# First layer's expert outputs stored by slot, and gathered per token in the second layer, in a two-layer graph network kernel

## The chip, the core and the metric

The kernel runs on one core of one Trainium2 chip. The core has a tensor engine for matrix products (PE), a vector engine (DVE), a scalar engine (ACT), a general engine (POOL), a sync engine that mostly starts transfers (SP), and 16 DMA engines that carry the transfers. The metric is the device time of one execution in microseconds (us); the median of several runs is compared. All data is float32 unless a line says otherwise.

## The reference, cut to what matters

625 nodes (called tokens here) with 768 features pass through two layers. Each layer adds a graph convolution and a linear-attention mix to x, and then a mixture-of-experts network in which each token goes to 2 of 8 experts:

```python
xn = _layernorm(x)
x = x + _L0_gnn_ref(xn, ...) + _L0_mix_ref(xn, ...)        # layer 0
x = x + _L0_ffn_ref(_layernorm(x), ...)                    # experts of layer 0
xn = _layernorm(x)
x = x + _L1_gnn_ref(xn, ...) + _L1_mix_ref(xn, ...)        # layer 1
x = x + _L1_ffn_ref(_layernorm(x), ...)
return x

def _L0_ffn_ref(x, Wg, bg, W1, b1, W2, b2, W3, b3):
    scores = x @ Wg + bg
    topk_vals, topk_idx = jax.lax.top_k(scores, 2)
    gates = softmax(topk_vals)
    comb = einsum('bnk,bnke->bne', gates, one_hot(topk_idx, 8))
    out = zeros_like(x)
    for e in range(8):
        h = gelu(x @ W1[e] + b1[e])          # 768 -> 192
        h = gelu(h @ W2[e] + b2[e])          # 192 -> 384
        y = h @ W3[e] + b3[e]                # 384 -> 768
        out = out + comb[..., e:e+1] * y
    return out
```

The change touches the last line of the expert network of layer 0, that is, how each token's two gated outputs y are added to x, and the first lines of layer 1, which take the layernorm of that sum.

## The kernel before

Tokens are kept as NB = 5 blocks of T = 125 rows. A list scheduler orders each engine's instructions; where the text of the program asks for it, the vector engine is kept in the written order (L1185 to `in_order.close` at L1211, ahead of the expert blocks). Every engine works through its own instructions strictly in that order.

The experts of layer 0 work on slots. The router chooses two experts per token, and `Dispatch` gives each of the 1250 token-expert pairs a slot: `two_i` holds, for each token, its two slot numbers. The slots form 21 blocks, each for one expert: 13 blocks of 128 rows (NPB = 13) and 8 half blocks of 64. The list `RUN` has the 13 blocks that always run (0 to 9 among the whole ones, and the half blocks 13, 14 and 15, with 9 the last); the list `MORE` has the other eight, which run only if the routing fills them (`tc.If`, L1339). With these inputs it does not.

A block (`block0`, or `block0_half` for half blocks) loads the expert's weights on the sync queue, gathers its tokens' rows from the DRAM tensor `tokens` by an indirect transfer on POOL's queue (L532, tile `xg`), transposes them, makes three matrix products with two activations between, and multiplies the result by the gate (L1274, L1324, tile `y`, 128 x 768). Then y is added into the DRAM tensor `sums`, row by row at its tokens' places, by an indirect transfer on POOL's queue that reads, adds and writes (`scatter_add`, L536). `sums` holds x with the expert biases already, stored at L1213. As every scatter reads and writes the same tensor, each waits for the one before it. Half blocks put their two column halves on partitions 0 to 63 and 64 to 127, so their y has 128 x 384 elements. Two blocks are in work at a time (`blocks0`), each doing a step in turn; tiles `y` are two.

Behind the blocks a few transposes of a matrix of edge counts run (L1347). Then layer 1 starts (L1360 to L1367). For each token block b, the sync queue loads its rows of `sums` into a tile `part` (`token_rows` L367, in two transfers of 112 and 13 rows; three such tiles take turns), a layernorm is done on DVE (L243 to L232), the tensor engine transposes the block (L187), ACT or DVE copies the columns out (L177, L175), a matrix product with the graph convolution's first weights follows (L201), and a second layernorm and its transposes feed the mix. Later in layer 1 the rows of `sums` are loaded once more (L1548), for the residual. The `tc.If` that stands between the two layers makes the first load of layer 1 wait for all that was begun before it, on every queue.

The second graph convolution of layer 0 runs its eight relations in a loop and calls `vectors_of_features(r)` at each; this loads small parameter rows at r = 0, and transposes them at r = 1.

Of the kernel before, what the change touches and what calls it, by code (L numbers as in the profile page):

```python
# [7 lines left out]
F32 = mybir.dt.float32  # L8
BF16 = mybir.dt.bfloat16
I32 = mybir.dt.int32  # L10
# [7 lines left out]
T = 125  # L18
NB = 5
NH = 313  # L20
NP = 2 * NH
HC = 314
D = 768
# [9 lines left out]
NPB = 13  # L33
NHB = 8
NS = NPB + NHB
RUN = (0, 1, 2, 13, 3, 4, 5, 14, 6, 7, 8, 15, 9)
MORE = (10, 11, 12, 16, 17, 18, 19, 20)
# [6 lines left out]
def kernel(ctx: ExitStack, tc: tile.TileContext, a: dict, out: bass.AP):  # L44
    nc = tc.nc

    const = ctx.enter_context(tc.tile_pool(name="const", bufs=1))
    wpool = ctx.enter_context(tc.tile_pool(name="wpool", bufs=5))
    rowp = ctx.enter_context(tc.tile_pool(name="rowp", bufs=3))
    small = ctx.enter_context(tc.tile_pool(name="small", bufs=2))  # L50
    psum = ctx.enter_context(tc.tile_pool(name="psum", bufs=4, space=PSUM))
    dram = ctx.enter_context(tc.tile_pool(name="dram", bufs=1, space=DRAM))
# [174 lines left out]
    def layernorm(src, dst, width, blocks=range(NB), into=None):  # L227

        into = into or blocks
        mv, r = moments(src, width, blocks)  # L230
        for i, b in enumerate(blocks):
            nc.vector.tensor_scalar(dst[:, into[i], :], src[:, b, :], mv[:, i, 0:1], r[:, i : i + 1],  # L232
                                    op0=OP.subtract, op1=OP.mult)
# [53 lines left out]
    class Router:  # L287
# [52 lines left out]
        def add_biases(self, x, pool):  # L340
# [10 lines left out]
            for bs in ((0, 1, 2), (3, 4)):  # L351
# [6 lines left out]
                for b in bs:  # L358
                    nc.vector.tensor_add(halves(x[:, b, :]), pss[b][:T, :, :384], halves(x[:, b, :]))

    def token_rows(dram_ap, tile_ap, store):

        for p in (slice(0, 112), slice(112, T)):
            if store:
                nc.sync.dma_start(dram_ap[p], tile_ap[p])
            else:
                nc.sync.dma_start(tile_ap[p], dram_ap[p])  # L367

    def by_token(d):
        return d[0 : N, :].rearrange("(b p) d -> p b d", p=T)  # L370

    class Dispatch:
# [7 lines left out]
        def __init__(self, pool, keep, router):  # L380
# [5 lines left out]
            for b in range(NB):  # L386
                n = NB - b
# [30 lines left out]
            nc.vector.tensor_reduce(two[:, 1, :], pos, AX.X, OP.max)  # L418
            nc.vector.tensor_reduce(two[:, 0, :], pos, AX.X, OP.add)
            nc.vector.tensor_sub(two[:, 0, :], two[:, 0, :], two[:, 1, :])  # L420
            two_i = pool.tile([T, 2 * NB], I32, name="d_twoi", bufs=1)
            nc.vector.tensor_copy(two_i, two.rearrange("p c b -> p (c b)"))
            part_i = pool.tile([T, 2, 2 * NB], I32, name="d_parti", bufs=1)
            nc.vector.tensor_single_scalar(part_i[:, 0, :], two_i, 127, op=OP.bitwise_and)
# [28 lines left out]
            for k, of in enumerate((slice(0, NPB), slice(NPB, NS))):  # L453
                n = of.stop - of.start
# [76 lines left out]
    def gather(dst, table_d, rows):  # L531
        nc.gpsimd.indirect_dma_start(out=dst, out_offset=None, in_=table_d,  # L532
                                     in_offset=bass.IndirectOffsetOnAxis(ap=rows, axis=0))

    def scatter_add(table_d, src, rows):
        nc.gpsimd.indirect_dma_start(out=table_d, out_offset=bass.IndirectOffsetOnAxis(ap=rows, axis=0),  # L536
                                     in_=src, in_offset=None, compute_op=OP.add)
# [10 lines left out]
    def half_rows(table_d):  # L548
        return table_d.rearrange("r (h d) -> (r h) d", h=2)


    sides = [slice(0, 64), slice(64, 128)]
# [38 lines left out]


    tokens_d = [dram.tile([SPARE + 128, D], F32, name=f"tokens{i}") for i in range(2)]
    sums_d = [dram.tile([SPARE + 128, D], F32, name=f"sums{i}") for i in range(2)]

    def over_degrees(r):
# [92 lines left out]
    with tc.tile_pool(name="big0", bufs=1) as big, ExitStack() as stack:  # L689
# [20 lines left out]
        with ExitStack() as phase:  # L710
# [85 lines left out]
            for hp in range(KC):  # L796
# [3 lines left out]
                for b0 in range(0, NB, 2):  # L800
                    n = min(2, NB - b0)
# [334 lines left out]
        with tc.tile_pool(name="rel2", bufs=1) as rel:  # L1136

            places = {}
            columns_of = {}

            def vectors_of_features(r):
                if r == 0:
                    many = places["all"] = rowp.tile([128, 1024], F32, name="row")
                    for c, (name, n, width) in enumerate((("L0_ffn_b1", 16, 96), ("L0_ffn_b2", 24, 128), ("L1_ffn_b1", 72, 128))):
                        nc.scalar.dma_start(many[:n, c * 128 : c * 128 + width], vector_rows(name, width))
                    at = 0
                    for name, n in (("L1_gnn_g1", 8), ("L1_gnn_be1", 8), ("L1_gnn_br1", 8), ("L1_mix_ln_in_g", KC),
                                    ("L1_mix_ln_in_b", KC), ("L1_mix_ln_out_g", KC), ("L1_mix_ln_out_b", KC)):
                        nc.scalar.dma_start(many[at : at + n, 384:512], vector_rows(name, 128))
                        places[name] = at  # L1150
                        at += n
                    places["n"] = at
                if r != 1:
                    return
                many, at = places.pop("all"), places.pop("n")
                ps = ps_tile()
                for c, (name, n, width) in enumerate((("fb1", 16, 96), ("fb2", 24, 128), ("gb1", 72, 128))):
                    nc.tensor.transpose(ps[:width, 0, c * 128 : c * 128 + n], many[:n, c * 128 : c * 128 + width], ident[:n, :n])
                    columns_of[name] = const.tile([width, n], F32, name=f"cols_{name}")
                    nc.vector.tensor_copy(columns_of[name], ps[:width, 0, c * 128 : c * 128 + n])  # L1160
                nc.tensor.transpose(ps[:, 0, 384 : 384 + at], many[:at, 384:512], ident[:at, :at])
                nc.vector.tensor_copy(vectors, ps[:, 0, 384 : 384 + at])

                for b in range(NB):
                    nc.gpsimd.dma_start(edges_d[b, :T, blk(b)], ident[:T, :T], accum_op=OP.add)

                far = rel.tile([T, NB], I32, name="far_i", bufs=1)
                nc.vector.tensor_scalar(far, token[:T], -1.0, None, op0=OP.mult)
                near = rel.tile([T, NB], I32, name="near_i", bufs=1)
                nc.vector.tensor_single_scalar(near, far, 127, op=OP.bitwise_and)  # L1170
                nf = rel.tile([T, NB], F32, name="near_f", bufs=1)
                nc.vector.tensor_copy(nf, near)
                nc.vector.tensor_scalar(token_parts[:, 1, :], nf, -1.0, None, op0=OP.mult)
                nc.vector.tensor_add(token_parts[:, 0, :], token[:T], nf)

            router = Router(0, "L0_ffn_Wg", "L0_ffn_bg", "L0_ffn_b3", None, None)

            def rows_done(x):
                t = token_place(work_place())
                router.rows_of = lambda b: (t, b)  # L1180
                router.tT = rel.tile([128, 18 * HC], F32, name="pair", bufs=1)[:, : KC * NP].rearrange("p (k n) -> p k n", k=KC)

                def one(b):
                    if b == NB - 1:
                        in_order.enter_context(tc.manual_schedule(engines={mybir.EngineType.DVE}))  # L1185
                    router.rows(x, b)
                    if b:
                        router.score(b - 1)

                return one  # L1190

            slabs_ = slab_tiles(a["L0_gnn_W2"][0], D, 3)
            nc.scalar.dma_start(by_token(aside_d[2]), x)
            x = rgcn(rel, parts, "L0_gnn_W2", False, {"cnt": cnt, "over": over, "w": slabs_}, lambda i: (work_place, features_place, x_place)[i](),
                     lambda: recall(2, x_place), vectors_of_features, rows_done)
            router.choose(0, NB - 1)
            router.score(NB - 1)
            router.choose(NB - 1, NB)
# [6 lines left out]
    with tc.tile_pool(name="msums", bufs=1) as msums:  # L1205
        msum = msums.tile([128, NB, DQ * 128], F32, name="msum")
        with tc.tile_pool(name="work0", bufs=2) as moe:
            places_of = Dispatch(moe, moe, router)
            idx, es_i, used = places_of.idx, places_of.es_i, places_of.used
# [20 lines left out]
            def block0(b, spare_pool=None):  # L1230
# [35 lines left out]
                y = moe.tile([128, D], F32, name="y")  # L1266
# [5 lines left out]
                if not gates:  # L1272
                    gates.extend(gate())
                nc.vector.tensor_scalar(halves(y), ps[:, :, :384], gates[0][:, b : b + 1], None, op0=OP.mult)  # L1274
                scatter_add(sums_d[0], y, idx[:, b : b + 1])

            def block0_half(b, w1, w2, w3):

                i = b - NPB
# [42 lines left out]
                if not gates:  # L1322
                    gates.extend(gate())
                nc.vector.tensor_scalar(y, ps[:, 0, :384], gates[1][:, i : i + 1], None, op0=OP.mult)  # L1324
                scatter_add(half_rows(sums_d[0]), y, places_of.idx2[:, i : i + 1])

            def blocks0(bs, spare_pool=None):

# [21 lines left out]
    with ExitStack() as phase:  # L1350
# [6 lines left out]
        nc.vector.memset(xnT[:, :, N:NP], 0.0)  # L1357
        xl = lay.tile([T, NB, 1024], F32, name="xl")

        for b in range(NB):  # L1360
            xb = part.tile([T, 1, D], F32, name="part", bufs=3)
            token_rows(by_token(sums_d[0])[:, b, :], xb[:, 0, :], False)
            layernorm(xb, xb, D, [0])
            block_to_columns(xb, xnT, KC, b, 0)
            evac(halves(xl[:, b, :]), token_matmul(xnT, w1_of, KC, b, 512), b)
            layernorm(xb, xb, D, [0])
            block_to_columns(xb, hT, KC, b, 0, (AF.Identity, places["L1_mix_ln_in_g"], places["L1_mix_ln_in_b"]))  # L1367
# [95 lines left out]
        nc.scalar.copy(halves(kvb), pkv[:, :, :384])  # L1463


        gT = lay.tile([128, 8, NP], F32, name="gT")
        arow = source_rows(al, 4)
        brow = row("L1_gnn_b1", 1024)
        wq = slabs(wqkv[:, 0:D], D, 3)
# [286 lines left out]
```

## Time and profile before

| | |
|---|---|
| runs | 2396.97, 2398.72, 2400.65 us; median 2398.72 |
| profiled execution | 2397.42 us; its span 2395.7 us; tensor engine clock granted 0.971 |
| PE busy | 2220.3 us, 93% of the span |
| DVE busy | 929.5 us, 39% |
| ACT busy | 277.8 us, 12% |
| POOL busy | 466.2 us, 19% |
| DMA | 311.21 MB in 152851 packets, 130 GB/s over the span |

The expert blocks of layer 0 take about 1360 to 1490 us of the span, the start of layer 1 about 1490 to 1580. In the rows of the profile, L532 is the line of the helper that issues the gathers, L536 that of the scatters, L367 that of the loads of token rows. "x26" is a number of instructions, and "idle before" the time that an engine waited just ahead of them, with what ended most of the wait. "SPq", "ACTq" and "POOLq" are the transfers that an engine issues, and "issue to landing" is the time from the issue until the data has arrived.

### The profile page before, as it was taken

To read this page: it belongs to the slowest core of one execution; us is meant where nothing else is said; L and a number is where in the kernel's file an instruction comes from. 1 tells how busy PE (TensorE), PEld (TensorE's weight loads), DVE (VectorE), ACT (ScalarE), POOL (GpSimd) and SP (SyncE) were. 2 spreads that over 40 slices of the span, in tenths; PEclk is the share of its full clock that TensorE was granted. 3 is DMA by queue.
4 is the path that set the end of the run, shared out by engine and by line. 5 is a ranking of instruction groups with operands and counts; after the bars stand their busy time and mean duration, and the time that the engine had idled before them with its cause. 6 is when DMAs were issued, how large, how long until landed. Compare 5 with 4: busy or idle time off the path is not lost. (4 is left out here: it accounts for less than half of the span.)

```text
span 2395.7 us, 25088 instructions
## 1 busy us (share of the span) xinstructions
PE 2220.3 (93%) x10262; PEld 1470.3 (61%) x10262; DVE 929.5 (39%) x1930; ACT 277.8 (12%) x579; POOL 466.2 (19%) x262
## 2 busy tenths in 40 slices
PE   7999989999999999999999687699999998699997
PEld 4666556777776567777776454355666555455554
DVE  7554133444343333443452521522765533511111
ACT  2111000000001100000000122211643200111110
POOL 1676533232220022222210021000000200011100
PEclk9999999999999999999999799899999999699999
DMA  9435395444422051111101699121003200679795
GB/s 357 96 54 56 67 273 136 121 129 130 126 76 79 7 191 59 64 59 54 34 1 52 207 301 280 39 73 72 1 1 131 73 13 13 248 296 358 285 391 195
DMA packets 152851, 311.21 MB, mean 130 GB/s; under 512 B 49087, under 2 KB 70723, under 8 KB 152689
## 3 DMA queue, kind: packets, MB, share of 16 engines
q1 hardware_dynamic: 91154, 232.46, 27.7%
q0 software_dynamic: 52208, 49.67, 10.5%
q10 hardware_dynamic: 9358, 27.30, 3.4%
q8 instruction: 87, 1.43, 0.2%
q14 instruction: 44, 0.35, 0.0%
HBM read 249.49 MB, written 63.58 MB: 131 GB/s over the span
## 5 line engine op out<-in xcount | busy, mean ns | idle before, releaser
L921 PE MATMUL ps<-cnt,parts 125*128 125x314 bf16 x2880 | 389.5, 298 | 9.8 <-DVEq L1107 8.4
L921 PEld LDWEIGHTS <-parts 125*128 125x128 bf16 x2880 | 282.1, 98 | 116.8 <-issue 11.1
L677 POOL DMA_INDIRECT table<-val,idx x80 | 159.6, 1996 | 131.0 <-DMA table<-val,idx 69.3
L969 PE MATMUL ps<-pair,w 128*128 128x314 f32 x504 | 137.5, 431 | 7.6 <-ACT pair L177 7.6
L943 POOL TENSOR_TENSOR features<-w 128x1152 f32<-128x1152 f32 x14 | 37.3, 2668 | 522.0 <-issue 348.0
L1624 PE MATMUL ps<-w,xT 128*128 128x384 f32 x360 | 126.2, 502 | 11.3 <-DVE xT L175 6.7
L969 PEld LDWEIGHTS ps<-pair,w 128*128 128x128 f32 x504 | 96.3, 191 | 46.1 <-ACT pair L177 8.1
L532 POOL DMA_INDIRECT xg<-tokens,d_idx x26 | 27.2, 1045 | 482.9 <-DVE gates L338 151.2
L1640 PE MATMUL ps<-w,hT 128*128 128x384 f32 x360 | 119.2, 487 | 0.0
L201 PE MATMUL ps<-w,hT 128*125 128x384 f32 x360 | 117.8, 486 | 0.0
L1624 PEld LDWEIGHTS ps<-w,xT 128*128 128x128 f32 x360 | 67.8, 195 | 56.2 <-DVE xT L175 8.2
L177 ACT COPY features<-ps 128x628 f32<-128x628 f32 (+1 forms) x15 | 10.5, 703 | 766.8 <-PE ps L921 766.0
L201 PEld LDWEIGHTS ps<-w,hT 128*125 128x125 f32 x360 | 67.1, 188 | 47.0
L1640 PEld LDWEIGHTS ps<-w,hT 128*128 128x128 f32 x360 | 67.5, 190 | 45.0
L1434 PE MATMUL ps<-xl,pT 125*125 125x256 f32 (+1 forms) x300 | 81.1, 427 | 12.4 <-ACT pT L177 8.8
L890 PE MATMUL ps<-w,features 128*125 128x384 f32 x240 | 82.9, 504 | 0.0
L975 DVE TENSOR_TENSOR pair<-ps,pair 128x628 f32<-128x628 f32 (+1 forms) x60 | 44.8, 746 | 97.5 <-PE ps L969 97.5
L1546 POOL TENSOR_TENSOR row<-row 128x768 f32<-128x768 f32 x1 | 2.1, 2094 | 395.7 <-DVE off L1412 395.7
L536 POOL DMA_INDIRECT sums<-y,d_idx x25 | 39.5, 1578 | 202.8 <-DMA sums<-y,d_idx 81.0
L201 PE MATMUL ps<-w,features 128*125 128x384 f32 x240 | 78.5, 487 | 0.0
L210 PE MATMUL ps<-features,w 128*128 128x313 f32 x288 | 77.4, 427 | 0.0
L1434 PEld LDWEIGHTS ps<-xl,pT 125*125 125x125 f32 x300 | 56.2, 191 | 34.2 <-ACT pT L177 10.3
(426 smaller groups left out, 3349.9 us busy)
## 6 DMA issues: line engine op xcount, KB each, us to landing
w<-in_L_ffn_w_dram SPq DMA_DIRECT2D x78, 1152.0 KB
w<-in_L_gnn_W_dram SPq DMA_DIRECT2D x34, 1152.0 KB
w<-in_L_ffn_W_dram SPq DMA_DIRECT2D x13, 1152.0 KB
table<-zero SPq DMA_DIRECT2D x32, 400.0 KB
cnt<-table POOLq DMA_DIRECT2D x16, 800.0 KB, 8.1
edges<-cnt POOLq DMA_DIRECT2D x8, 1600.0 KB, 16.3
w<-in_L_ffn_W_dram SPq DMA_DIRECT2D x13, 576.0 KB
w<-in_L_mix_W_qkv_dram SPq DMA_DIRECT2D x6, 1152.0 KB
```

Of the source, the lines that this page charges most:

```text
L201: nc.tensor.matmul(ps[:T, h, :width], xT[:, k, blk(b)], w_of(k)[:, h * width : (h + 1) * width], start=(k == 0), stop=(k == nk - 1))
L210: nc.tensor.matmul(ps[:width, h, :NH], w_of(k)[:, c0 : c0 + width], xT[:, k, h * NH : (h + 1) * NH], start=(k == 0), stop=(k == nk - 1))
L536: nc.gpsimd.indirect_dma_start(out=table_d, out_offset=bass.IndirectOffsetOnAxis(ap=rows, axis=0), in_=src, in_offset=None, compute_op=OP.add)
L677: scatter = nc.gpsimd.indirect_dma_start(out=table_of(g, j), out_offset=bass.IndirectOffsetOnAxis(ap=idx[:, j : j + 1], axis=0), in_=val[: ...
L890: nc.tensor.matmul(ps[:T, h, :384], aggs[:, k, blk(b)], w_of(k)[:, h * 384 : (h + 1) * 384], start=(k == 0), stop=(k == KC - 1))
L921: nc.tensor.matmul(ps[:, h, :HC], parts[:, b, i, k * 128 : (k + 1) * 128], cnt[:T, b, h * HC : (h + 1) * HC], start=(b == 0 and i == 0), s ...
L943: nc.gpsimd.tensor_add(wmix[:, 1], b11, b12)
L969: nc.tensor.matmul(ps[:, j, :HC], right[:, k, c : c + 128], left(k), start=(k == 0), stop=(k == K2 - 1))
L975: nc.vector.tensor_add(total, ps[:, :n, :HC], total)
L1434: nc.tensor.matmul(o, pT[:, j, :], xl[:, j, cols], start=(j == 0), stop=(j == NB - 1))
L1624: nc.tensor.matmul(ps[:, 0, :384], xT[:, k, :], w1_of(k)[:, q * 384 : (q + 1) * 384], start=(k == 0), stop=(k == KC - 1))
L1640: nc.tensor.matmul(ps[:, h, :384], hT[:, k, :], w2_of(k)[:, h * 384 : (h + 1) * 384], start=(k == 0), stop=(k == 8))
```

## The change

In layer 0 each block's y is no longer added into `sums`. It is stored, by a plain transfer, to a new DRAM tensor `rows` with one row per slot (21 x 128 rows of 768). Whole blocks use one transfer of 128 rows, half blocks two of 64 rows and 384 columns, all on POOL's queue, but for the last block, which uses ACT's queue. As tokens' slots may lie anywhere, the rows of blocks and half blocks that are not written are filled with zeros before, at r = 2 of the second graph convolution of layer 0: one DVE instruction makes a tile of zeros, and eight transfers of 384 KB and three of 192 KB on ACT's queue store it. The tile of slot numbers is kept from the dispatch (`slots_of`).

At the beginning of layer 1, for each token block b, the row of x with biases is loaded from `sums`, two indirect gathers of 125 rows each on POOL's queue bring the two slots' rows, two additions on DVE make the sum, and two transfers on the sync queue store it back to `sums` for the later reload; the first layernorm then works on the sum. These tiles take turns in two places (`b % 2`), in the space of the tile `gT`, which is needed only later and is now allocated flat. The `part` tiles receive the layernorm's output.

```diff
--- before.py
+++ after.py
@@ -358,6 +358,9 @@
                 for b in bs:
                     nc.vector.tensor_add(halves(x[:, b, :]), pss[b][:T, :, :384], halves(x[:, b, :]))
 
+
+    slots_of = const.tile([T, 2 * NB], I32, name="slots_of")
+
     def token_rows(dram_ap, tile_ap, store):
 
         for p in (slice(0, 112), slice(112, T)):
@@ -418,7 +421,7 @@
             nc.vector.tensor_reduce(two[:, 1, :], pos, AX.X, OP.max)
             nc.vector.tensor_reduce(two[:, 0, :], pos, AX.X, OP.add)
             nc.vector.tensor_sub(two[:, 0, :], two[:, 0, :], two[:, 1, :])
-            two_i = pool.tile([T, 2 * NB], I32, name="d_twoi", bufs=1)
+            two_i = slots_of
             nc.vector.tensor_copy(two_i, two.rearrange("p c b -> p (c b)"))
             part_i = pool.tile([T, 2, 2 * NB], I32, name="d_parti", bufs=1)
             nc.vector.tensor_single_scalar(part_i[:, 0, :], two_i, 127, op=OP.bitwise_and)
@@ -591,6 +594,8 @@
 
 
     tokens_d = [dram.tile([SPARE + 128, D], F32, name=f"tokens{i}") for i in range(2)]
+
+    rows_d = dram.tile([NS * 128, D], F32, name="rows")
     sums_d = [dram.tile([SPARE + 128, D], F32, name=f"sums{i}") for i in range(2)]
 
     def over_degrees(r):
@@ -1150,6 +1155,15 @@
                         places[name] = at
                         at += n
                     places["n"] = at
+                if r == 2:
+
+                    none = rowp.tile([128, 1024], F32, name="row")
+                    nc.vector.memset(none[:, :D], 0.0)
+                    for b in MORE:
+                        nc.scalar.dma_start(rows_d[b * 128 : (b + 1) * 128, :], none[:, :D])
+                    for b in RUN:
+                        if b >= NPB:
+                            nc.scalar.dma_start(rows_d[b * 128 + 64 : (b + 1) * 128, :], none[:64, :D])
                 if r != 1:
                     return
                 many, at = places.pop("all"), places.pop("n")
@@ -1272,7 +1286,7 @@
                 if not gates:
                     gates.extend(gate())
                 nc.vector.tensor_scalar(halves(y), ps[:, :, :384], gates[0][:, b : b + 1], None, op0=OP.mult)
-                scatter_add(sums_d[0], y, idx[:, b : b + 1])
+                (nc.scalar if b == RUN[-1] else nc.gpsimd).dma_start(rows_d[b * 128 : (b + 1) * 128, :], y)
 
             def block0_half(b, w1, w2, w3):
 
@@ -1322,7 +1336,8 @@
                 if not gates:
                     gates.extend(gate())
                 nc.vector.tensor_scalar(y, ps[:, 0, :384], gates[1][:, i : i + 1], None, op0=OP.mult)
-                scatter_add(half_rows(sums_d[0]), y, places_of.idx2[:, i : i + 1])
+                for j, p in enumerate(sides):
+                    nc.gpsimd.dma_start(rows_d[b * 128 : b * 128 + 64, j * 384 : (j + 1) * 384], y[p])
 
             def blocks0(bs, spare_pool=None):
 
@@ -1357,10 +1372,18 @@
         nc.vector.memset(xnT[:, :, N:NP], 0.0)
         xl = lay.tile([T, NB, 1024], F32, name="xl")
 
+
+        sixth = lay.tile([128, 8 * NP], F32, name="gT")[:T, : 6 * D].rearrange("p (i a d) -> p i a d", i=2, a=3)
         for b in range(NB):
             xb = part.tile([T, 1, D], F32, name="part", bufs=3)
-            token_rows(by_token(sums_d[0])[:, b, :], xb[:, 0, :], False)
-            layernorm(xb, xb, D, [0])
+            three = sixth[:, b % 2]
+            token_rows(by_token(sums_d[0])[:, b, :], three[:, 0, :], False)
+            for c in range(2):
+                gather(three[:, 1 + c, :], rows_d, slots_of[:, c * NB + b : c * NB + b + 1])
+            for c in range(2):
+                nc.vector.tensor_add(three[:, 0, :], three[:, 0, :], three[:, 1 + c, :])
+            token_rows(by_token(sums_d[0])[:, b, :], three[:, 0, :], True)
+            layernorm(three[:, 0:1, :], xb, D, [0])
             block_to_columns(xb, xnT, KC, b, 0)
             evac(halves(xl[:, b, :]), token_matmul(xnT, w1_of, KC, b, 512), b)
             layernorm(xb, xb, D, [0])
@@ -1463,7 +1486,7 @@
         nc.scalar.copy(halves(kvb), pkv[:, :, :384])
 
 
-        gT = lay.tile([128, 8, NP], F32, name="gT")
+        gT = lay.tile([128, 8 * NP], F32, name="gT").rearrange("p (k n) -> p k n", k=8)
         arow = source_rows(al, 4)
         brow = row("L1_gnn_b1", 1024)
         wq = slabs(wqkv[:, 0:D], D, 3)
```

## The prediction

> **What bounds the kernel now.** I read the page's first rows, then the rows of the two kinds of indirect transfer that the change touches, then the timeline where layer 0 hands over to layer 1, and last the waits of the sync queue and the windows there.
>
> ```profile
> PE 2220.3 (93%) x10262; PEld 1470.3 (61%) x10262; DVE 929.5 (39%) x1930; ACT 277.8 (12%) x579; POOL 466.2 (19%) x262
> L532 POOL DMA_INDIRECT xg<-tokens,d_idx x26 | 27.2, 1045 | 482.9 <-DVE gates L338 151.2
> L536 POOL DMA_INDIRECT sums<-y,d_idx x25 | 39.5, 1578 | 202.8 <-DMA sums<-y,d_idx 81.0
> ...
> table<-val,idx POOLq DMA_INDIRECT x80, 4.2
> xg<-tokens,d_idx POOLq DMA_INDIRECT x26, 8.1
> sums<-y,d_idx POOLq DMA_INDIRECT x25, 9.0
> ```
>
> PE is busy 93% of the span, so only what opens or closes a hole in PE's work can move the end. The scatters take 39.5 us of POOL and POOL waits twice that for their landings, but POOL is no bound: these rows matter only where PE stands behind them. There are two such places, inside layer 0's expert blocks and at the hand-over:
>
> ```profile
> 1482.51 0.55 PE L1221 MATMUL ps<-ident,a 128*128 128x128 f32 x3 [1.29 <-DVE a L1262]
> ...
> 1489.44 1.02 DVE L1274 TENSOR_SCALAR y<-ps,d_gate 128x768 f32<-128x768 f32 x1 [6.99 <-PE ps L1270]
> 1489.78 1.55 POOL L536 DMA_INDIRECT sums<-y,d_idx  x1 [6.26 <-DMA sums<-y,d_idx]
> ...
> 1497.26 1.56 POOL L536 DMA_INDIRECT sums<-y,d_idx  x1 [5.93 <-DMA sums<-y,d_idx]
> 1504.54 2.46 SPq L367 DMA_DIRECT2D part<-sums  x6
> ...
> 1508.06 1.02 DVE L243 BATCH_NORM_STATS2 ln_st<-part 125x6 f32<-125x384 f32 x2 [2.68 <-DMA part<-sums]
> ...
> 1511.41 0.86 PE L187 MATMUL ps<-ident,part 125*128 125x125 f32 x3 [17.25 <-DVE part L232]
> ```
>
> The last block's y is ready at 1490.46. Its scatter stands behind the one before it (issued 1489.78) until 1497.26 and lands just before 1504.54, when the first load of sums is issued. The load lands 3.5 us later, the first layernorm takes 3.3 us, and PE goes on at 1511.41 after a hole of 17.25 us. That hole is the prize.
>
> ```profile
> SPq L367 <- DMA sums<-y,d_idx: 7.7, 1, 7.7
> ...
> 1490.00:1495.00 5.00, 2.96 (x25) 2.80 (x25) 0.46 (x1) 2.99 (x5) 1.32 (x1) 1.00 0.92 270
> 1495.00:1497.00 2.00, 0.00 (x0) 0.00 (x0) 0.00 (x0) 1.31 (x2) 0.00 (x0) 1.00 0.15 25
> 1512.00:1580.00 68.00, 59.96 (x172) 28.73 (x171) 39.47 (x148) 15.15 (x38) 0.00 (x0) 0.96 0.06 16
> ```
>
> The first line (sync queue's waits) says that the last scatter alone held the load 7.7 us: all else that it waits for was there at about 1496.8. The windows (last two columns: busy share of the DMA engines, GB/s) say why not sooner: the weight slab and the scatters keep the DMA engines at 0.92 until 1495. In 1512-1580 PE works 59.96 of 68 us with DVE at 39.47, so DVE has room, but not at every moment.
>
> **The change, step by step** (negative is gained).
>
> 1. Blocks. The 13 chained scatters become plain stores, each waiting for its own y only. DVE's waits for a free y tile end; of these PE felt 1.29 us at 1482.51 and 0.85 at 1473.44. A store still holds its tile until it lands, so I take some 60%: -1.3. Ends: 0, if stores land no sooner; -3, if the last block's matmuls at L1270 (5.83 us for 12 against about 4.0 in earlier blocks) also quicken. Stores issue on POOL at 1-1.5 us like the scatters (1578 ns); the three half blocks add few, and POOL has room. The last block's store goes through ACT's queue, where nothing urgent stands behind it (the layernorm's root comes later).
>
> 2. Last y to the first load. Before: 15.1 us (1489.44 to 1504.54). After: the store needs no second turn, and the load waits for the slab too, until about 1496.3 (DMA share 0.92 falling to 0.15): 6.9 us, so -8.2. It cannot be better than the slab. If the store takes 9.0 us like a scatter, it lands at 1499.8: -4.7.
>
> 3. First load to PE's restart. Before 6.87 us. After, POOL issues four gathers (b=0, 1) behind the same gate. Each costs 1.045 us by the L532 row plus some 0.3, so the fourth is issued at 3.9. In the changed program's order DVE adds both gathers of b=1 before it ends the layernorm of b=0: behind the fourth landing are an add (0.96, as 125x768 adds cost here) and the tail L218 to L232 (1.7), 2.7 in all. So restart = 3.9 + L + 2.7, L from issue to landing. No gather of 125 rows of 3 KB is in the trace; rows near it:
>
> ```profile
> 1260.00:1274.00 14.00, 14.00 (x110) 10.69 (x108) 0.00 (x0) 2.73 (x4) 0.00 (x0) 1.00 0.33 130
> 1275.20 4.42 DVE L1008 TENSOR_TENSOR x<-ps,x 125x768 f32<-125x768 f32 x5 [17.27 <-DMA x<-aside]
> ```
>
> Here a load onto 125 partitions runs alone, with 0.33 of the 16 engines busy at 130 GB/s, and DVE waits 17.27 us for it. [...] With the row: 384 KB at 130 GB/s is 3.0 us of moving, and with the 4.2 us of the 125-row scatters of 256 bytes (whose own moving I put at 0.7) L = 6.5. If only the 128-row gathers were the measure, moving would be 1.0-1.3 and L = 4.4 to 5. I take the row with 125 partitions, rounded to 6.6: it has the gather's shape. Restart 13.2, so +6.3; by 16 engines (L = 5.0) +4.7. Ends: L = 4.4 (+4.1) and 9.0, the scatters' median under load (+8.7).
>
> 4. b=2 and 3. Their buffers are the two of b=0 and 1, so their gathers start when L232 of those is through: at the restart P, and about P+5.1. The last lands at P+5.1+1.3+6.6 = P+13.0; its adds stand in DVE's order ahead of the copy of b=1's columns that PE needs, which came at P+16.6 before. With DVE's backlog I put that copy at P+18.5: +1.9. Ends: 0.5 and 4. Five blocks have ten adds, 9.6 us of DVE; the rest fits in PE's matmuls (10.5 to 12.6 us per block). Ten SP stores back to sums are needed only at the reload L1548, long after; SP issues them at 0.37 us each, and its next weight loads come at 1577, when they are through.
>
> 5. The zero-fill (3.7 MB, one memset, 11 stores on ACT's queue) comes at about 928-955 in the second relational convolution. ACT has no work there and DMA is mostly idle; behind it on ACT's queue stand a row of degrees and a load of counts that are needed at about 1014. The cover is some 60 us; cost 0. If that cover were gone: 3.7 MB at 300 GB/s, +12 at most; I see nothing that takes it away. The flat allocation of gT, and keeping the slot numbers in a constant tile: 0.
>
> Sum: -1.3 - 8.2 + 6.3 + 1.9 = -1.3. The profiled execution took 2397.42 us (span 2395.7 and 1.7 around it), 1.3 below the median of 2398.72. Taken off the median: 2397.4. With the 16-engine figure (4.7, and 1.0 in step 4) it would be -3.8: 2394.9.
>
> **Rivals.**
>
> A, likeliest: as summed, the hole is half refilled, -4 to +3.
>
> B, the gathers are quick and the adds are hidden: L = 4.4, step 4 at zero, step 1 at -3: -3 - 8.2 + 4.1 = -7.1, so 2391.6. For it: DMA is nearly idle after 1496 (0.15, then 0.06). Against it: the 125 rows.
>
> C, on the other side: the transfers land late. In the trace both xg and sums have medians over 8 us. The sum is 2L - 14.5 (L stands in step 3 and again in step 4), so it turns at L = 7.2 us, and passes +4.8 at 9.6. At L = 9.0 it is +3.5; if the last store takes 9.0 too, step 2 gives only -4.7, and the total is +7.0: 2405.7. For it: the four gathers and two loads run together, and DVE's in-order queue passes every late landing to PE. Against it: the medians are from a stage with the DMA engines full.
>
> D: the change does not do what it says: the first load is held as long by something else, and the time of 1504.5 stays. The 7.7 us wait names the scatter only, so I give this little, and count it with C.
>
> **How the numbers follow.** 0.2% (4.8 us) is about what a measurement of this kernel can tell from no change. A 0.45: mostly within it (0.32), 0.08 faster, 0.05 slower. B 0.25: faster. C with D 0.30: slower 0.27, within 0.03. Faster 0.33, same 0.35, slower 0.32. The range goes from B's 2391.6 less 2 to C's 2405.7 plus 2; A's own is 2394 to 2402.
>
> **What would show it.** Right: first load of layer 1 at about 1496 instead of 1504.5; gathers from issue to landing 6 to 7 us; PE's restart 13 us after the first load; in the following 70 us PE's busy time per us slightly lower than 59.96/68. Wrong: landings over 9 us or near 4.5 (C or B), a first load not earlier than 1500 (C or D), ACT's rows of degrees late after 955 with a hole in PE near 1014, or a PE hole at b=2 and 3 of over 5 us, which would be a longer DVE backlog than step 4 has.

## Result: slower by a third of a percent, and the profile after

The changed kernel takes 2405.89 us (median of 10 runs, 2400.24 to 2408.21), the kernel before 2398.41 us beside it. The ratio is 1.0033, with a 95% interval of 1.0022 to 1.0044. The profiled execution took 2405.28 us, span 2403.5.

First the page of the changed kernel, busy time by engine. Lines after L362 have moved: the gathers are now L535, the additions L1384, the loads L370, the stores back L368.

```profile
PE 2230.1 (93%) x10262; PEld 1477.3 (61%) x10262; DVE 941.5 (39%) x1941; ACT 278.0 (12%) x579; POOL 466.1 (19%) x274
```

PE has the same 10262 instructions, yet it is busy 9.8 us longer, so some of its work has become slower: 3.5 us of it lie between 1512 and 1570 us, but 5.7 us lie before 400 us, where the edit changes nothing, so the sum alone says little. The waits at the sync queue between 1470 and 1560 (in total, times, longest):

```profile
SPq L368 <- DVE gT L1384: 10.5, 2, 7.9
SPq L368 <- DMA gT<-sums: 8.4, 3, 3.9
```

The scatter waits are gone from the sync queue; it now waits for additions on DVE before it can store back. Next, the timeline from the last y of layer 0 to PE's restart.

```profile
1485.04 1.02 DVE L1288 TENSOR_SCALAR y<-ps,d_gate 128x768 f32<-128x768 f32 x1 [5.30 <-PE ps L1284]
...
1494.43 1.64 SPq L370 DMA_DIRECT2D gT<-sums  x4
...
1495.39 1.26 POOL L535 DMA_INDIRECT gT<-rows,slots_of  x1 [16.65 <-DMA gT<-sums]
...
1500.01 1.21 POOL L535 DMA_INDIRECT gT<-rows,slots_of  x1 [0.30 <-issue]
1502.54 0.96 DVE L1384 TENSOR_TENSOR gT<-gT 125x768 f32<-125x768 f32 x1 [8.26 <-DMA gT<-rows,slots_of]
1503.79 1.21 POOL L535 DMA_INDIRECT gT<-rows,slots_of  x1 [2.57 <-DVE gT L1384]
1504.77 0.96 DVE L1384 TENSOR_TENSOR gT<-gT 125x768 f32<-125x768 f32 x1 [1.28 <-DMA gT<-rows,slots_of]
...
1508.27 0.96 DVE L1384 TENSOR_TENSOR gT<-gT 125x768 f32<-125x768 f32 x1 [0.21 <-DMA gT<-rows,slots_of]
...
1510.87 1.49 PE L187 MATMUL ps<-ident,part 125*128 125x125 f32 x6 [16.98 <-DVE part L232]
```

The last y comes 4.4 us sooner and the first load 10.1 us sooner (1494.43 against 1504.54), so the prize is there. But the restart is only 0.5 us sooner. Block 0's two additions wait for their gathers until 1502.54 and 1504.77. From there DVE is at work with hardly a pause, and block 1's two additions stand ahead of the end of block 0's layernorm; the last of them, fed by the fourth gather (issued 1500.01), starts at 1508.27 after a wait of 0.21 us. Up to here the change gains half a microsecond. The loss comes in the 40 us after that. First the three products of blocks 0, 1 and 2 in the kernel before, then the changed kernel:

```profile
1513.98 12.59 PE L201 MATMUL ps<-w,x 128*125 128x512 f32 x24 [1.09 <-ACT x L177]
...
1529.03 10.56 PE L201 MATMUL ps<-w,x 128*125 128x512 f32 x24 [1.18 <-DVE x L175]
...
1543.20 10.56 PE L201 MATMUL ps<-w,x 128*125 128x512 f32 x24 [2.32 <-ACT x L177]
```

```profile
1511.62 5.64 SPq L370 DMA_DIRECT2D gT<-sums  x4
...
1513.44 12.99 PE L201 MATMUL ps<-w,x 128*125 128x512 f32 x24 [1.09 <-ACT x L177]
...
1520.11 0.96 DVE L1384 TENSOR_TENSOR gT<-gT 125x768 f32<-125x768 f32 x1 [4.17 <-DMA gT<-sums]
...
1531.56 0.93 DVE L175 COPY x<-ps 128x750 f32<-128x750 f32 x1
...
1532.55 11.98 PE L201 MATMUL ps<-w,x 128*125 128x512 f32 x24 [4.83 <-DVE x L175]
...
1548.13 12.26 PE L201 MATMUL ps<-w,x 128*125 128x512 f32 x24 [2.32 <-ACT x L177]
```

DVE's first addition for block 2 (1520.11) stands 4.17 us idle for a load of x rows that was issued at 1511.62, and everything behind it on DVE is late, the copy of block 1's columns at 1531.56 too. PE waits 4.83 us for that copy; before it waited 1.18 there. Then the product of block 1 takes 11.98 us and that of block 2 12.26, where both took 10.56 before. The windows of the changed kernel say why. They are cut where the granted clock changes; the trace gives it in stretches of 3.41 us or multiples of that. The first number in a row behind the length is PE's busy time, and the last three are the granted clock, the share of the DMA engines and GB/s:

```profile
1528.60:1532.02 3.42, 0.00 (x0) 0.00 (x0) 2.70 (x13) 2.15 (x5) 0.00 (x0) 1.00 0.69 236
1532.02:1535.43 3.41, 2.88 (x4) 1.32 (x5) 3.35 (x14) 1.43 (x5) 0.00 (x0) 0.50 0.06 22
...
1545.67:1549.08 3.41, 1.09 (x4) 0.48 (x3) 3.40 (x13) 2.70 (x7) 0.00 (x0) 1.00 0.01 2
1549.08:1552.50 3.42, 3.42 (x6) 1.34 (x5) 2.51 (x15) 0.00 (x0) 0.00 (x0) 0.50 0.00 0
```

PE does nothing in the stretch to 1532.02, and in the next one its granted clock is half; it is half once more from 1549.08, behind a stretch in which PE was idle for 2.32 of 3.41 us. So the stage has these terms against the kernel before: 3.65 us more waiting at block 1, 1.42 and 1.70 us of half clock in the products of blocks 1 and 2, 0.40 in that of block 0. That is 7.2 us, less the 0.5 gained at the restart: 6.7. The same PE instructions compared one by one are 0.4 us sooner at 1451 us and 6.6 to 6.9 us later from 1560 to 2380 us, so the loss is made there, and none of it is given back or added later but for about one microsecond at the ends of the span.

### The profile page after: what moved, and what is told of

It is laid out like the page before. It is cut to its first block, busy times and chain, and to the rows that moved or that the text cites. A ratio compares the mean times of both kernels' runs of the same rounds, so it can differ in the third digit from the quotient of the medians.

```text
span 2403.5 us, 25159 instructions
## 1 busy us (share of the span) xinstructions
PE 2230.1 (93%) x10262; PEld 1477.3 (61%) x10262; DVE 941.5 (39%) x1941; ACT 278.0 (12%) x579; POOL 466.1 (19%) x274
## 5 line engine op out<-in xcount | busy, mean ns | idle before, releaser
L535 POOL DMA_INDIRECT xg<-tokens,d_idx x26 | 27.6, 1062 | 486.9 <-DVE gates L338 151.2
L1457 PEld LDWEIGHTS ps<-xl,pT 125*125 125x125 f32 x300 | 55.9, 190 | 34.3 <-ACT pT L177 10.3
L974 PE MATMUL ps<-x,w 128*128 128x314 f32 x252 | 69.6, 435 | 3.8 <-DVE x L956 2.2
```

The source lines that it names most:

```text
L974: nc.tensor.matmul(ps[:, j, :HC], right[:, k, c : c + 128], left(k), start=(k == 0), stop=(k == K2 - 1))
L1457: nc.tensor.matmul(o, pT[:, j, :], xl[:, j, cols], start=(j == 0), stop=(j == NB - 1))
```

## Experiments

**e1: the plain stores alone.** The beginning of layer 1 is put back as it was.

```diff
-            three = sixth[:, b % 2]
-            token_rows(by_token(sums_d[0])[:, b, :], three[:, 0, :], False)
-            for c in range(2):
-                gather(three[:, 1 + c, :], rows_d, slots_of[:, c * NB + b : c * NB + b + 1])
-            for c in range(2):
-                nc.vector.tensor_add(three[:, 0, :], three[:, 0, :], three[:, 1 + c, :])
-            token_rows(by_token(sums_d[0])[:, b, :], three[:, 0, :], True)
-            layernorm(three[:, 0:1, :], xb, D, [0])
+            token_rows(by_token(sums_d[0])[:, b, :], xb[:, 0, :], False)
+            layernorm(xb, xb, D, [0])
```

> The changed kernel with the plain stores by slot and the zero-fill, but with the old beginning of layer 1: no gathers, no additions, no stores back. It leaves out that the experts' outputs of layer 0 are added, so layer 1 works on other numbers. All theories agree that the whole loss of the change lies behind the first load of layer 1. So the last y and the first load should come as in the changed kernel (y at 1485, load at 1494.4 on the trace's scale), the restart 6.9 us after the load (about 1501.5), and the tensor engine should then meet no hole over 2.5 us in the five blocks. Against the kernel before: about -10 us, 2388 to 2390. If the zero-fill or the stores have a price of their own upstream, it would be less, -7 or so.

Layer 1 works on other numbers here, and PE has 10998 instructions instead of 10262, so the total (2570.15 us) cannot be compared; the profile up to the experts of layer 1 can. The first load comes at 1495.53 and PE restarts at 1502.47, 6.9 us later, with no hole over 2.4 us in the five blocks; against the kernel before, PE's instructions stand 1.0 us later at 1451 and 8.3 us sooner at 1612. So stores, zero-fill and the shorter hand-over are worth about 9 us, and the gathering costs 16.

**e2: gathers of 128 rows.** Three rows are fetched for nothing.

```diff
-    slots_of = const.tile([T, 2 * NB], I32, name="slots_of")
+    slots_128 = const.tile([128, 2 * NB], I32, name="slots_of")
+    nc.vector.memset(slots_128, 0)
+    slots_of = slots_128[:T]
...
-            three = sixth[:, b % 2]
+            all_rows = sixth[:, b % 2]
+            three = all_rows[:T]
...
-                gather(three[:, 1 + c, :], rows_d, slots_of[:, c * NB + b : c * NB + b + 1])
+                gather(all_rows[:, 1 + c, :], rows_d, slots_128[:, c * NB + b : c * NB + b + 1])
```

> The changed kernel with gathers of 128 rows in place of 125 (three rows are fetched for nothing). Theory 'few engines': the gathers of 125 rows run on 5 DMA engines and land 7 to 8.5 us after issue; with 16 engines they land in about 5 to 6, the restart comes 2 to 3 us sooner, the later loads find free engines, and the total falls by 4 to 8 us against the changed kernel (2398 to 2402). Theory 'order on DVE': additions for blocks 2 and 3 stand ahead of the copy that PE needs and wait for the loads of x, which are issued only after the layernorm of block 0; then 128 rows give only the 2 us at the restart or less, and the hole of 4.8 us at block 1 stays over 3 us (2403 to 2405).

Measured: 2397.75 us, ratio to the kernel before 1.0001 (0.9985 to 1.0017), so about 8 us less than the changed kernel. Its timeline:

```profile
1494.38 1.01 POOL L537 DMA_INDIRECT gT<-rows,slots_of  x1 [15.74 <-DVE far L1425]
1495.70 0.98 POOL L537 DMA_INDIRECT gT<-rows,slots_of  x1 [0.30 <-issue]
...
1499.84 0.96 DVE L1387 TENSOR_TENSOR gT<-gT 125x768 f32<-125x768 f32 x1 [5.64 <-DMA gT<-rows,slots_of]
1501.68 0.96 DVE L1387 TENSOR_TENSOR gT<-gT 125x768 f32<-125x768 f32 x1 [0.89 <-DMA gT<-rows,slots_of]
```

The first two gathers reach DVE 5.5 and 6.0 us after their issue, against 7.2 and 7.8 us in the changed kernel (issued 1495.39 and 1496.96, added at 1502.54 and 1504.77). The first one is also issued with the load and not 0.96 us behind it. A stretch of each trace in which gathers alone move data, first the changed kernel and then e2 (last two numbers: share of the 16 DMA engines, GB/s):

```profile
1500.50:1505.50 5.00, 0.00 (x0) 0.00 (x0) 1.69 (x2) 0.00 (x0) 1.93 (x2) 0.50 0.70 196
...
1500.00:1502.50 2.50, 0.00 (x0) 0.00 (x0) 1.61 (x2) 0.00 (x0) 0.95 (x1) 0.50 0.94 356
```

Counted in the trace's records of packets, those of 4 and 8 bytes left out, 5.0 are in flight while one gather of 125 rows moves (1499.0 to 1499.5), 10.6 between 1500.5 and 1505.5, and 16.2 with 128 rows. The restart is 12.8 us after the load instead of 16.4, DVE's wait for block 2's row of x falls from 4.17 to 1.30 us, the wait at block 1 is 1.45 us, and no product after the first is slow. The theory of few engines predicted this. The theory of the order on DVE did not, though the order was left as it was: DVE's instructions follow each other as in the changed kernel. So the additions ahead of the copy cost little when the transfers are early.

**e3: the order on DVE alone.** The transfers keep their 125 rows; `prepare` holds the loads, gathers, additions, store and layernorm of a block.

```diff
+        prepare(0)
         for b in range(NB):
+            xb = xbs[b]
             block_to_columns(xb, xnT, KC, b, 0)
+            if b + 1 < NB:
+                prepare(b + 1)
...
+                behind(nc.vector.tensor_add(three[:, 0, :], three[:, 0, :], three[:, 1 + c, :]))
```

> The changed kernel with one thing different: on DVE the additions of block b+1 are kept behind the layernorm of block b (for b=0) and behind the copy of block b's columns (for odd b), so no addition of a later block can hold the copy that PE waits for. Transfers are the same, 125 rows. Theory 'order on DVE': restart 1.5 to 2 us sooner than in the changed kernel (about 1509), no hole over 2.5 us at blocks 1 and 2, hence no half clock there either: 6 to 9 us less than the changed kernel, 2397 to 2400. Theory 'few engines': the transfers still come late, and the waits move to the layernorm of blocks 2 and 3: 0 to 3 us less than the changed kernel.

Measured: 2398.18 us, ratio 1.0007 (0.9993 to 1.0022), as the theory of the order said.

```profile
1524.66 0.94 DVE L175 COPY x<-ps 128x750 f32<-128x750 f32 x1
1525.51 0.95 DVE L1386 TENSOR_TENSOR gT<-gT 125x768 f32<-125x768 f32 x1
...
1525.65 1.12 PE L201 MATMUL ps<-w,x 128*125 128x512 f32 x2 [1.19 <-DVE x L175]
```

The addition of block 2 now stands behind the copy, PE waits 1.19 us instead of 4.83, and both slow products take 10.56 us again. The restart is 14.5 us after the load, 1.9 us sooner than in the changed kernel, as much as block 1's two additions take.

**e4: the rows of x loaded early.** The additions of blocks 2 and 3 still stand ahead of the copy on DVE.

```diff
+        for b in range(NB):
+            token_rows(by_token(sums_d[0])[:, b, :], xl[:, b, :D], False)
...
-            token_rows(by_token(sums_d[0])[:, b, :], three[:, 0, :], False)
...
-                nc.vector.tensor_add(three[:, 0, :], three[:, 0, :], three[:, 1 + c, :])
+            with tc.issue_after(done["ln"].ins) if b in (2, 3) else tc.issue_after(done["copy"].ins) if b == 4 else ExitStack():
...
+                    nc.vector.tensor_add(xl[:, b, :D], xl[:, b, :D], two[:, c, :])
```

> The changed kernel with the rows of x of all five blocks loaded at once at the beginning (into the tile xl, which is free until each block's product), the additions on DVE kept in the changed kernel's order. Theory 'late loads of x': the additions of block 2 waited 4.2 us for a load that was issued at 1511.6 only and landed at 1520; with the rows there, they start at about 1516, the copy of block 1's columns is back in time, the hole of 4.8 us falls to 2 us or less and the half clock behind it goes: 4 to 7 us less than the changed kernel (2399 to 2402). Theory 'few engines' or 'too much on DVE': the additions of block 3 still wait for gathers that land at 1518 to 1520, and the hole stays over 3 us: 0 to 2 us less.

Measured: 2406.06 us, ratio 1.0032 (1.0019 to 1.0046): nothing gained. The profile shows both halves of the account.

```profile
1487.82 4.43 SPq L371 DMA_DIRECT2D xl<-sums  x10
1488.57 1.27 POOL L536 DMA_INDIRECT gT<-rows,slots_of  x1 [16.75 <-DVE far L1432]
...
1502.35 0.96 DVE L1388 TENSOR_TENSOR xl<-xl,gT 125x768 f32<-125x768 f32 x1 [14.68 <-DMA gT<-rows,slots_of]
...
1543.35 12.15 PE L201 MATMUL ps<-w,x 128*125 128x512 f32 x24 [2.32 <-ACT x L177]
```

The wait at block 1 falls from 4.83 to 1.19 us and no addition of blocks 2 and 3 waits, so the late load of x was what held the additions. But the first gather now reaches DVE 13.8 us after its issue, with ten loads (1.9 MB) in flight beside it, and the restart is 22.7 us after the load instead of 16.4. What is won at block 1 is lost at block 0. My expectation had looked at block 1 alone. The profiled execution is the quickest of the twelve (2398.60 us): PE was 7.4 us ahead of the kernel before at 1451 us already. From there to 1580 us it loses 9.1 us, the changed kernel 7.1. And block 2's product is slow here too, without a hole at block 1.

**e5: both cures.** e2 and e3 together.

> The order on DVE of e3 and the 128 rows of e2 together. If the two cures remove the same loss (the hole at block 1 and the half clock behind it), they do not add: what is left to gain is the restart, where the second gather lands some 7.3 us after the first load (e2) and only one pair of additions and the layernorm follow, about 11.6 us after the load against 12.8 (e2) and 14.5 (e3). Total 1 to 2 us under e2, about 2396. If they are two losses of their own, the sum is -15 from the changed kernel, 2391.

Measured: 2395.87 us, ratio 1.0001 (0.9988 to 1.0013). The cures do not add up: for the most part both take away the same loss. The stage by itself shows it more closely than the total. From 1451 to 1580 us PE's instructions fall behind the kernel before by 7.1 us in the changed kernel, and gain 2.5 us on it in e2, 1.8 in e3 and 4.5 in e5, one profiled execution each: against the changed kernel 9.5, 8.9 and 11.6 us. The total hides a part of this. In the traces of e2 and e5 PE loses 2.9 and 3.1 us between 2020 and 2040 us, where the clock is at half for 6.83 us and is not in those of the kernel before, the changed kernel and e3; whether other executions have this is not known. The restart comes 12.6 us after the load, no better than in e2; the microsecond that I expected from the order is not there, since the first addition still starts only 6.9 us after the load.

**e6: one place instead of two.** In e5, `sixth[:, b % 2]` becomes `sixth[:, b % 1]`, so that block 1's transfers wait for block 0.

> As e5, but the three tiles of a block have one place instead of two, so that the loads and gathers of block 1 are issued only when block 0 is through with it. Theory 'transfers of block 1 slow those of block 0': with half the data in flight the gathers of block 0 land about 1 us sooner and the restart comes at 10.5 us after the load: 1 us under e5. The later blocks have 10 us of room each, as their additions stand behind the copy anyway. Rival: the restart does not move, since the two gathers of block 0 are ahead on POOL's queue; then block 1 is late (its load is issued at the restart, lands 3.5 us later, gathers earlier) and the time is that of e5 or up to 3 us more.

Measured: 2393.98 us, ratio 0.9989 (0.9975 to 1.0003). The first addition starts 4.8 us after the load (1500.17 and 1495.39) and the restart comes at 10.2 us, as the theory of competing transfers said. With it the change is not a proven gain either.

**e7: the kernel before, with two tensors of sums.** Every second block is scattered into another tensor, and a plain load and one addition per block join them.

```diff
+            def place_of(b):
+
+                return other_d if b in RUN and RUN.index(b) % 2 else sums_d[0]
...
-                scatter_add(sums_d[0], y, idx[:, b : b + 1])
+                scatter_add(place_of(b), y, idx[:, b : b + 1])
...
+            token_rows(by_token(sums_d[0])[:, b, :], two[:, 0, :], False)
+            token_rows(by_token(other_d)[:, b, :], two[:, 1, :], False)
+            nc.vector.tensor_add(two[:, 0, :], two[:, 0, :], two[:, 1, :])
```

> The kernel before, with every second block of RUN scattered into a second tensor of sums (zeros before, filled at r = 2 on ACT's queue), so that a scatter waits for the one before the last only. At the beginning of layer 1 both tensors' rows are loaded on the sync queue (112 and 13 rows each), one addition per block on DVE, stored back as in the change. If the prize at the hand-over lies in the wait of the last scatter for the one before it, the first load comes 6 to 8 us sooner than before (about 1497 to 1498), the restart 8 to 9 us after it (one more load beside, one addition), and the total is 4 to 7 us under the kernel before: 2391 to 2394. If scatters that read and write are slow by themselves under load (9 us), the first load comes at 1500 or later and the gain is 2 us or none.

Measured: 2391.73 us, ratio 0.9978 (0.9964 to 0.9992), the lowest median of all and the only interval wholly below 1.

```profile
1488.45 1.57 POOL L536 DMA_INDIRECT sums<-y,d_idx  x1 [7.12 <-DVE y L1284]
1497.83 0.84 SPq L367 DMA_DIRECT2D gT<-sums  x2
```

The last scatter is issued as soon as its y is there, the first load comes at 1497.83, 6.7 us sooner than before, and PE restarts at 1508.09, 10.3 us after it.

**e8: work in PE's hole.** Ten products that nobody reads are put ahead of block 1's product in the changed kernel.

```diff
+            if b == 1:
+                idle = ps_tile()
+                for i in range(10):
+                    behind(nc.tensor.matmul(idle[:T, 0, :512], xnT[:, 0, blk(0)], w1_of(0)[:, :512], start=True, stop=True))
```

> The changed kernel with ten extra matrix products (128 x 125 by 128 x 512, into a place that nobody reads) that fill the hole of 4.8 us which PE has ahead of block 1's product. The work ahead on DVE and the transfers are the same, so the copy that PE waits for comes as late as before. Theory 'the hole halves the clock': with PE busy in the hole, block 1's product takes 10.6 us instead of 12.0, and perhaps block 2's 10.6 instead of 12.3: 1.4 to 3.1 us less than the changed kernel, although work is added. If the half clock comes from something else (the loads, the general rhythm), both products stay at 12 and the time is the changed kernel's or up to 1 us more.

```profile
1531.92 8.75 PE L1391 MATMUL ps<-w,x 128*125 128x512 f32 x20
1540.50 10.46 PE L201 MATMUL ps<-w,x 128*125 128x512 f32 x24
...
1554.57 10.56 PE L201 MATMUL ps<-w,x 128*125 128x512 f32 x24 [2.32 <-ACT x L177]
```

The products of blocks 1 and 2 are back at 10.46 and 10.56 us. For block 1 this shows that the hole was behind the half clock. For block 2 it does not: e4 has no hole at block 1, and its block 2 is at half clock all the same (12.15 us). What decides there is how the gap of 2.32 us ahead of block 2 lies against the stretches of 3.41 us. These are the stretches around that gap, with PE's busy time first and the granted clock third from the end, in the kernel before, in e4 and in e8:

```profile
1538.57:1541.98 3.41, 2.31 (x15) 1.54 (x13) 2.31 (x5) 1.70 (x5) 0.00 (x0) 1.00 0.21 46
1541.98:1545.39 3.41, 2.19 (x5) 1.04 (x6) 3.20 (x15) 1.16 (x3) 0.00 (x0) 1.00 0.17 67
...
1539.76:1543.17 3.41, 1.27 (x12) 1.03 (x10) 3.38 (x6) 2.74 (x7) 0.00 (x0) 1.00 0.01 2
1543.17:1546.58 3.41, 3.23 (x4) 1.50 (x5) 3.33 (x21) 0.42 (x2) 0.00 (x0) 0.50 0.00 0
...
1550.60:1554.01 3.41, 1.65 (x13) 1.21 (x11) 3.01 (x5) 2.36 (x7) 0.00 (x0) 1.00 0.01 2
1554.01:1557.43 3.42, 2.86 (x7) 1.42 (x8) 3.37 (x20) 0.80 (x2) 0.00 (x0) 1.00 0.02 5
```

Every trace has this gap. In the changed kernel, e4 and e9, 2.14 to 2.32 us of it lie in one stretch, and the clock is at half in the next. In the other eight the gap is split, with at most 1.79 us in one stretch, and no half clock follows. The stretches lie differently in each execution, so the 1.70 us that the changed kernel lost at block 2 were an accident of the execution that was profiled. I estimate that the hole of 4.83 us has no such luck: wherever it lies, one stretch has at least half of it, 2.4 us, more than the 2.14 us that half clock followed here.

I mis-sized the filler: ten products are twenty instructions and take 8.75 us, more than the hole, so the total is 2408.15 us (ratio 1.0051, 1.0034 to 1.0068), and the time that I expected did not come. (Its profiled execution was the longest of the six, 2413.74 us; only the stage is read from it.)

**e9: no stores back.** The line with `True` is dropped from the changed kernel.

> The changed kernel without the ten stores back to sums. It leaves out that the residual of layer 1 has the experts' outputs of layer 0, so what follows the reload works on other numbers; it is read up to 1600 us only. Theory 'transfers compete': without the stores (750 KB of the first two blocks) the loads of x for blocks 2 and 3 land sooner, at about 1517 instead of 1520, and the hole at block 1 falls from 4.8 to about 2. Theory 'order on DVE and the late issue': the loads are issued at 1511.6 in any case (after the layernorm of block 0), and the gathers of blocks 2 and 3 alone keep the engines busy: the hole stays over 3.5 us.

```profile
1516.21 0.96 DVE L1384 TENSOR_TENSOR gT<-gT 125x768 f32<-125x768 f32 x1 [2.67 <-DMA gT<-sums]
...
1529.23 11.98 PE L201 MATMUL ps<-w,x 128*125 128x512 f32 x24 [4.00 <-DVE x L175]
```

The addition of block 2 starts at 1516.21 after a wait of 2.67 us, and the hole at block 1 is 4.00 us, again with a product of 11.98 us behind it. With the stores this addition starts 9.2 us after the restart (1520.11 and 1510.87), without them 7.0 (1516.21 and 1509.19), so they make the loads later, but they are not what makes most of the hole. Its total (2583.54 us, one run) is not comparable.

## Why the prediction was wrong

It forecast -1.3 us and called a change within 0.2% the likeliest; the time rose by 7.5 us, which my range just held at its upper end. Step by step:

1. Blocks, -1.3: the last y is 4.4 us sooner. The sign was right and the size too small: the last products of the stage took 4.14 us instead of 5.83, which I had as an end of the range.
2. Last y to first load, -8.2: measured -5.7 (9.4 us instead of 15.1). The first two steps together are -10.1 against -9.5. Why the load did not come sooner stays open: the DMA engines' share is down to 0.03 between 1492 and 1494, and no run tried what else held it.
3. Load to restart, +6.3: measured +9.6. The path was right, its terms too small. The first gather was issued 1.0 us after the load, each took 1.5 us of POOL instead of 1.35, and the fourth reached DVE 8.3 us after its issue instead of 6.6. The choice of the load with 125 partitions as the measure was right: one gather of 125 rows has 5.0 packets in flight, and e2 with 128 rows (16.2 in flight) has 5.5 and 6.0 us where the changed kernel has 7.2 and 7.8. No run shows the 16-engine figure (L = 5.0) for 125 rows; the first gather of 128 rows reached DVE after 5.5 us in e2 and after 4.7 in e6, where only block 0's two were under way. But I had priced one gather alone, and four are in flight with loads.
4. Blocks 2 and 3, +1.9 with ends of 0.5 and 4: measured +7.2. This is the step that failed, and twice. I let the additions wait for gathers that start at the restart or later; the gathers of blocks 2 and 3 were issued before it, from 1503.79 on, and the additions waited for the load of x, which SP issues only after block 0's layernorm (1511.62) and which reached DVE 8.5 us later, not 3.5. So PE waited 3.65 us longer. And I priced PE's wait only and put what follows it at nothing: 3.1 us of half clock, 1.4 behind the hole and 1.7 by the accident at block 2, and 0.4 us in block 0's product. The place was right (additions ahead of the copy on DVE); e3 shows that moving them is enough, and e2 that faster gathers are enough too. Rival C had the late landings as its mechanism, but its sum has the same gap. That its +7.0 lies so near the measured 7.5 is luck: it has the blocks and the first load together at -6.0, measured -10.1, and the rest at +13.0, measured +16.8.
5. Zero-fill, 0: right. Compared one by one, PE's instructions keep the same distance to the kernel before, 1.12 us, from about 896 to 1257 us, and the fill lies between.

What I left out is what PE's granted clock does behind an idle stretch. The hole of 4.83 us covers the stretch to 1532.02 whole, and the clock is 0.50 in the next. At block 2 a whole idle stretch was not needed: 2.32 idle us of 3.41 were followed by 0.50 too, and 1.70 us were lost. As the stretches lie differently in each trace, the same gap had no half clock behind it in the eight traces where at most 1.79 us of it lay in one stretch.

What stays open is how often other executions of the changed kernel have the half clock at block 2, as only one was profiled. How the 16 engines share the gathers and loads in flight was not tried by itself.

## What to carry to other kernels

A stall that is taken away at a hand-over is worth only what the new way costs less: here 10 us of earlier start were spent on gathers, and more was lost on additions that stood ahead of a copy on DVE (PE waited 4.83 us for it, and 1.19 in e3, where they stand behind it). Ask of each late transfer which instruction waits for it, what is queued behind that one, and whether the tensor engine's clock falls behind the wait (here to 0.50, and 1.42 us were lost). A chain of read-add-write transfers was shortened by a second accumulator here, without gathers (e7: the first load 6.7 us sooner, the total 0.2% less).

## What the runs showed of the hardware

- Four indirect gathers of 125 rows of 3 KB reached DVE 7.2, 7.8, 8.5 and 8.3 us after their issue; of 128 rows, in the same place of the program, the first two did 5.5 and 6.0 us after it. One gather of 125 rows had 5.0 packets in flight, gathers of 128 rows 16.2.
- With ten loads of x in flight a gather took 13.8 us instead of 7.2 (e4).
- Behind a hole of 4.83 us PE's product took 11.98 us instead of 10.56, at a granted clock of 0.50 in the first stretch; behind one of 4.00 us it took 11.98 too (e9). With the hole filled it took 10.46 (e8).
- In the traces of both kernels the granted clock holds for 3.41 us or a multiple of that. A gap of 2.32 us was followed by half clock where 2.14 us or more of it lay in one stretch of 3.41 (changed kernel 12.26 us for the product, e4 12.15, e9 12.26), and not where at most 1.79 us did (10.56 in the kernel before and seven runs).
